# A two-layer graph kernel on one core: VectorE reads TensorE's results at later places in its order

## The chip, the core and the metric

The kernel runs on one core of a Trainium2 chip. A core has five engines that work beside each other: TensorE (PE in the profile; PEld is its weight load), VectorE (DVE), ScalarE (ACT), GpSimd (POOL) and SyncE (SP, which issues DMAs). Each engine runs its own instructions in order and waits, at an instruction, for semaphores of the others. The metric is the device time of one execution in microseconds. Three timed runs of the kernel before gave 2594.83 us as median (2593.11 to 2597.05).

## What is computed

The reference takes 3125 nodes with 256 features, 103125 edges sorted by destination (with self loops), and two layers. Cut to its end:

```python
xn = _layernorm(x, axis=-1)
x = x + _L0_gnn_ref(xn, src, dst, ...) + _L0_mix_ref(xn[None], ...)[0]
x = x + _L0_ffn_ref(_layernorm(x, axis=-1)[None], ...)[0]
xn = _layernorm(x, axis=-1)
x = x + _L1_gnn_ref(xn, src, dst, edge_type_8, ...) + _L1_mix_ref(xn[None], ...)[0]
x = x + _L1_ffn_ref(_layernorm(x, axis=-1)[None], ...)[0]
return x
```

- `_L0_gnn_ref` takes, for each node, the maximum over its incoming edges of a linear map of the source row. `_L0_mix_ref` is a linear attention: `q` and `k` have their mean over the features taken off, are squared and normalised; `kv` is a sum over all nodes. `_L0_ffn_ref` routes all tokens to the same two of eight experts (one decision from the mean of all rows), with a layer norm behind.
- `_L1_gnn_ref` sums, for each node, rows of the table "node x relation" over its edges. `_L1_mix_ref` is another linear attention. `_L1_ffn_ref` is a mixture of eight experts in which every token takes two; the kernel computes all eight and weighs each with a share that is zero for six of them.

## The kernel before

**Tiles and passes.** The nodes are sorted by their number of edges and cut into 25 tiles of 128. For tile `t`, `STEPS[t]` gathers fetch one source row for each of its 128 nodes; there are 814 gathers in a pass. `edge_pass` (L1241 and on) is run twice. Pass 1 (layer 0, maximum) gathers from `btab`, pass 2 (layer 1, sum) from `htab_f`. Ahead of pass 1 lies a stage that sorts and builds tables; between the passes lies the table stage (`Four`), which ends layer 0 and writes `htab_f`.

**What a pass does.** POOL issues the gathers (L179) in chunks of up to four into tiles `gt` from a pool of 6 (pass 1) or 5 (pass 2) buffers. VectorE folds a chunk (L1264) and adds it to the tile's accumulator (L1269; L1267 for a tile's first chunk). This frees the buffer for POOL.

**The order of everything else.** A queue `bg` holds jobs with a cost each. After each chunk the pass gives itself credit, a rate times the number of gathers, and takes jobs off `bg` while there is credit. The rate is the cost in `bg` by the gathers left in the group of tiles, held between the two values of `pace`. The order of VectorE's and POOL's instructions is exactly that of the program (`manual_schedule`); TensorE's and ScalarE's are placed by the scheduler, so a job's matmuls can begin before VectorE gets to the job's own instructions. But where a VectorE instruction needs a product, everything behind it on VectorE waits too, the folding of gathers among it.

**The jobs of pass 1.** First the mixing: `nodes_in` normalises five tiles, `mix_tile` is a generator with four stages (products; means and squares; sums over nodes; scaling and transposes), of which `mix_step(i)` runs one stage of each of four tiles, `i-3` to `i`. At the end of each group of tiles (`GROUPS`, mostly three tiles) `after0` appends that group's `Fin0` jobs (end of the first sublayer: `products`, `sums`, `norms`). From group 3 (`SURE`) on, when the two experts have been guessed from the nodes seen so far (`guess`), it also appends `hidden` (first expert matmuls and gelus), `outputs_a` (second matmuls, into one PSUM bank `py` for a tile) and `outputs_b`. The last lets ScalarE copy the first expert's half out of `py` (L1452), and VectorE add the second's to the token row and take it off the copy (L1453, L1454). `settle` later finds the true weights.

**The jobs of pass 2.** First attention: `att_k`, `att_softmax`, 25 times `att_ctx`, then `att_end`, in which VectorE reads the sum `pctx` (L1981). Then for each group of tiles a `Group`: ten small jobs (sums, norms, routing), ten jobs `step(i)` for the eight experts, and an end. `step(i)` runs `hidden(i)` (matmuls L2120, gelus L2124, and L2126, which spreads the row of shares of expert `i` over the partitions in PSUM, `wb`), `share(i-1)` (VectorE multiplies the gelus by `wb`, L2134) and `outputs(i-2)` (L2149). A group's last three steps and its end are dealt out between the first small jobs of the next group (`late`).

Of the kernel before, what the change touches and what calls it, by code (L numbers as in the profile page):

```python
# [11 lines left out]
F32 = mybir.dt.float32  # L12
# [44 lines left out]
SEEN = GROUPS[SURE][-1]  # L57

# [18 lines left out]
def gps_kernel(ctx: ExitStack, tc: tile.TileContext, a, out):  # L77
# [1155 lines left out]
    def fast():  # L1233
# [168 lines left out]
        hTs, pys = {}, {}  # L1402
# [41 lines left out]

        def outputs_b(ts):


            for t in ts:
                py = pys.pop(t)
                y = py.rearrange("p (i c n) -> p i c n", i=2, c=2)  # L1450
                d = xT[:, :, t * P : (t + 1) * P]
                S.copy(d, y[:, 0, :, :])  # L1452
                V.tensor_tensor(xt_tok[:, t, :], xt_tok[:, t, :], py[:, D:], op=ALU.add)  # L1453
                V.tensor_tensor(d, d, y[:, 1, :, :], op=ALU.subtract)  # L1454
# [12 lines left out]
        with ExitStack() as l0x:  # L1467
# [48 lines left out]
            w_qkv = mat_load("w_qkv", a["m0_qkv"], m0w, 3 * D)  # L1516
            b_qkv = row_load("b_qkv", a["m0_bqkv"], 3 * D, m0w)
# [5 lines left out]
            def nodes_in(g):  # L1523

                ask(5 * g + 5)
                yield
                mv = small.tile([P, 5, 2], F32, name="mv5")
                rs = small.tile([P, 5], F32, name="rs5")
                fetch(5 * g + 5)
                for j in range(5):  # L1530
                    stats(x[:, 5 * g + j, :], mv[:, j, :])
                V.tensor_scalar(rs, mv[:, :, 1], EPS, None, op0=ALU.add)
                S.activation(rs, rs, AF.Sqrt)
                yield
                V.reciprocal(rs, rs)
                for j in range(5):
                    xn = work.tile([P, D], F32, name="xn")
                    normalize(xn, x[:, 5 * g + j, :], mv[:, j, :], rs[:, j : j + 1])
                    to_xT(5 * g + j, xn)
# [5 lines left out]
            def mix_tile(t):  # L1545
# [7 lines left out]
                tok_mm(pvv[:, :D], w_qkv[:, :, 512:], t, stop=False)  # L1553
                PE.matmul(pvv[:, :D], ones_row, b_qkv[:, 512:], start=False, stop=True)
                yield
                nm = small.tile([P, 2], F32, name="nm")
                V.reduce_sum(nm, pq.rearrange("p (h d) -> p h d", h=2), axis=AX.X)
                V.tensor_scalar(nm, nm, -1.0 / D, None, op0=ALU.mult)
                ss = small.tile([P, 2], F32, name="ss")
                q2 = m0.tile([P, D], F32, name="q2", bufs=3)  # L1560
                k2 = m0.tile([P, D], F32, name="k2", bufs=3)
                S.activation(q2, pq[:, :D], AF.Square, bias=nm[:, 0:1], accum_out=ss[:, 0:1])
                S.activation(k2, pq[:, D:], AF.Square, bias=nm[:, 1:2], accum_out=ss[:, 1:2])
                vs = m0.tile([P, D], F32, name="vs", bufs=3)
                S.copy(vs, pvv[:, :D])
# [129 lines left out]
            nodes = [staged(nodes_in(g), (1.0, 4.0, 6.0)) for g in range(5)]  # L1695
# [3 lines left out]
            def mix_step(i):  # L1699
                for back in (3, 2, 1, 0):  # L1700
                    if 0 <= i - back < NT:
                        next(mixing[i - back], None)

            for i in range(NT + 3):
                bg.append((7.0 if i < NT else 3.0, lambda i=i: mix_step(i)))
                if i % 5 < 3 and i // 5 + 1 < 5:
                    bg.append(nodes[i // 5 + 1][i % 5])
            bg.extend(staged(mix_end(), (2.0, 3.0, 1.0)))

            def after0(g, tiles, accs):  # L1710
# [5 lines left out]
                if g == SURE:  # L1716
                    bg.extend(staged(guess(), (2.0, 1.0, 1.0, 1.0, 1.0, 1.0)))
                    for r in range(NX):
                        bg.extend(staged(relation(r), (1.5, 1.5)))
                for ts in GROUPS[: g + 1] if g == SURE else [tiles] if g > SURE else []:  # L1720
                    bg.append((5.0 * len(ts), lambda ts=ts: hidden(ts)))
                    bg.append((4.0 * len(ts), lambda ts=ts: outputs_a(ts)))
                    bg.append((1.0 * len(ts), lambda ts=ts: outputs_b(ts)))
# [4 lines left out]
            fin = []  # L1728
# [8 lines left out]
            with tc.manual_schedule(engines={mybir.EngineType.DVE, mybir.EngineType.Pool}):  # L1737
                edge_pass(
                    gp, btab[:], idx1, ALU.max, bg, after0, GROUPS, 4, (1.3, 1.3), None,
                    lambda t: accp.tile([P, D], F32, name="acc"), ahead,  # L1740
                )
                while bg:
                    bg.popleft()[1]()
# [3 lines left out]
            with tc.manual_schedule(engines={ET.DVE, ET.Pool, ET.PE, ET.Activation}):  # L1747
# [10 lines left out]
                outputs_a(ts)  # L1758

        again = nc.values_load(missed[0:1, 0:1])  # L1760
        with tc.If(again > 0):
# [8 lines left out]
            for ts in GROUPS:  # L1770
# [10 lines left out]
                outputs_a(ts)  # L1781
                if ts != GROUPS[-1]:
                    outputs_b(ts)
# [114 lines left out]
        with ExitStack() as l1x:  # L1898
# [101 lines left out]
            class Group:  # L2000
# [113 lines left out]
                def hidden(self, e):  # L2114
                    n, at0 = self.n, self.at0
                    hT = self.hT[e] = f1.tile([P, FC, 4 * P], F32, name="hT1")
                    for f in range(FC):
# [6 lines left out]
                        S.activation(hT[:, f, :n], ph[:, :n], AF.Gelu, bias=b1[:, e, f : f + 1])  # L2124
                    wb = self.wb[e] = ps_tr.tile([P, 512], F32, name="pt")
# [54 lines left out]
                def step(self, i):  # L2180

                    if i < NX:
                        self.hidden(i)
                    if 1 <= i <= NX:
                        self.share(i - 1)
# [39 lines left out]
            for t in range(NT):  # L2225
                bg.append((1.7, lambda t=t: att_ctx(t)))
                if t % 5 == 0:
                    bg.append((0.0, lambda e=t // 5: load_expert(e, wp)))
            bg.append((6.0, att_end))
# [120 lines left out]
```

## Time and profile before

| | us |
|---|---|
| timed median of 3 | 2594.83 |
| the profiled execution's own time | 3147.58 |
| its span | 3145.9 |
| first and last gather of pass 1 | 128.5, 1463.4 |
| first and last gather of pass 2 | 1716.6, 3056.2 |
| POOL busy, VectorE busy, TensorE busy | 1767.0, 1272.5, 1950.3 |

The profiled execution took 553 us more than the timed ones, so lengths read from it are its own and are not those of a timed run. In the lines of the profile a group of instructions is named by line, engine, operation and tiles; "[32.04 <-DVE acc L1269]" means that the engine was idle for 32.04 us ahead of the instruction, and that VectorE's result of line 1269 came last. "issue" is idle time in which nothing was waited for that the profile shows, and "remote" is a releaser that it can't name. The granted clock of TensorE averages 0.764 of full speed.

### The profile page before, as it was taken

What the parts mean: (1) busy time and instruction counts of PE and PEld (TensorE: products, weight loads), DVE (VectorE), ACT (ScalarE), POOL (GpSimd) and SP (SyncE); (2) the same over time, 40 slices, a digit from 0 to 9 for tenths busy, and PEclk for the clock granted to TensorE, in tenths of its full rate; (3) what the DMA queues carried; (4) which work ended last, traced back from release to release, by engine and by line L of the source; (5) the groups of instructions that cost most, each with busy time, mean ns of one, the idle gap of its engine ahead of it and who ended that gap; (6) DMA issues with size and microseconds to landing.
All of it is one profiled execution on the core that took longest, in us unless ns stands there. A gap on an engine that the chain in (4) does not pass through costs nothing.

```text
span 3145.9 us, 20994 instructions
## 1 busy us (share of the span) xinstructions
PE 1950.3 (62%) x6146; PEld 1123.0 (36%) x6146; DVE 1272.5 (40%) x3135; ACT 543.2 (17%) x1272; POOL 1767.0 (56%) x1850
## 2 busy tenths in 40 slices
PE   2446577205553515256897155587887788787888
PEld 1323243103332303134343144232333344554667
DVE  5635445336224232224552233443534254343442
ACT  2213220001110101012121131111212021221233
POOL 4365656675656474742344737675556655565650
PEclk8668777557766757577898567688988889888979
DMA  5332323233222232321478533232222222232220
GB/s 162 103 93 81 94 74 107 88 103 100 87 80 84 61 102 62 103 62 35 186 300 308 157 95 93 88 98 84 77 76 87 87 82 84 78 90 81 81 73 15
DMA packets 129367, 314.68 MB, mean 100 GB/s; under 512 B 39520, under 2 KB 64166, under 8 KB 122836
## 3 DMA queue, kind: packets, MB, share of 16 engines
q0 software_dynamic: 86784, 252.60, 26.8%
q1 hardware_dynamic: 36526, 56.36, 5.1%
q10 hardware_dynamic: 5926, 4.21, 0.5%
q8 instruction: 53, 0.87, 0.1%
q14 instruction: 78, 0.64, 0.1%
HBM read 246.35 MB, written 66.69 MB: 100 GB/s over the span
## 4 chain that ended last, share of the span: by engine, by line
PE 26%; issue 9%; another core or an unknown queue 6%; DVE 5%; DMA 3%; POOL 3%; ACT 2%; ACTq 0%; POOLq 0%; DVEq 0%
PE mm L2120 9%; PE py L2149 8%; PE mm L174 4%; POOL gt L179 2%; DMA htab_f<-hs,id_i 2%; PE pt L2126 2%; DVE gt L1264 1%; PE mm L2089 1%; DVE bnst L148 1%; PE mm L2014 1%; ACT L2124 0%; ACT hT L2124 0%; DVE acc L1269 0%; PE pt L2082 0%
## 5 line engine op out<-in xcount | busy, mean ns | idle before, releaser
L179 POOL DMA_INDIRECT gt<-htab_f,idx2g x814 | 797.5, 980 | 527.4 <-DVE acc L1269 269.7
L179 POOL DMA_INDIRECT gt<-btab,idx x814 | 799.9, 983 | 510.6 <-issue 224.7
L1264 DVE TENSOR_TENSOR gt<-gt 128x256 f32<-128x256 f32 (+1 forms) x831 | 444.4, 535 | 334.6 <-DMA gt<-btab,idx 149.8
L2120 PE MATMUL mm<-xT,w 128*128 128x256 f32 (+4 forms) x1408 | 403.6, 437 | 87.9 <-issue 63.4
L2149 PE MATMUL py<-hT,w 128*128 128x256 f32 (+4 forms) x1408 | 407.4, 439 | 78.2 <-issue 77.1
L2120 PEld LDWEIGHTS mm<-xT,w 128*128 128x128 f32 x1408 | 253.4, 208 | 233.4 <-issue 155.1
L2149 PEld LDWEIGHTS py<-hT,w 128*128 128x128 f32 x1408 | 250.5, 205 | 228.1 <-issue 187.6
L2134 DVE TENSOR_TENSOR hT<-hT,pt 128x1024 f32<-128x1024 f32 (+4 forms) x88 | 117.5, 1336 | 422.8 <-ACT hT L2124 241.1
L2124 ACT ACTIVATE hT<-mm,b 128x256 f32<-128x256 f32 (+4 forms) x352 | 167.9, 496 | 677.6 <-PE mm L2120 234.6
L1411 PE MATMUL mm<-xT,w 128*128 128x384 f32 (+2 forms) x320 | 125.1, 556 | 155.9 <-issue 110.3
L174 PE MATMUL mm<-w_rel,xT 128*128 128x512 f32 x400 | 183.6, 618 | 5.1 <-ACT xT L169 3.3
L1269 DVE TENSOR_TENSOR acc<-acc,gt 128x256 f32<-128x256 f32 x403 | 172.2, 427 | 35.0 <-DVE gt L1264 13.2
L174 PE MATMUL pt<-w_own,xT 128*128 128x256 f32 x100 | 44.4, 580 | 207.5 <-issue 113.8
L1411 PEld LDWEIGHTS mm<-xT,w 128*128 128x128 f32 x320 | 72.0, 251 | 208.9 <-issue 139.5
L1453 DVE TENSOR_TENSOR xt<-xt,mm 128x256 f32<-128x256 f32 x25 | 10.5, 420 | 308.1 <-ACT xT L1452 302.3
L1440 PE MATMUL mm<-w,hT 128*128 128x256 f32 x400 | 105.4, 413 | 29.1 <-issue 27.3
L174 PE MATMUL mm<-w_qkv,xT 128*128 128x512 f32 (+1 forms) x200 | 96.0, 596 | 41.7 <-issue 41.5
L174 PEld LDWEIGHTS mm<-w_rel,xT 128*128 128x128 f32 x400 | 77.9, 198 | 103.0 <-issue 87.1
L174 PEld LDWEIGHTS pt<-w_own,xT 128*128 128x128 f32 x100 | 25.6, 285 | 222.8 <-issue 121.1
L1440 PEld LDWEIGHTS mm<-w,hT 128*128 128x128 f32 x400 | 79.2, 204 | 66.9 <-issue 53.9
L1674 PE MATMUL pmean<-ones,xt 128*128 128x1 f32 (+1 forms) x100 | 23.5, 339 | 115.9 <-DVE xt L157 70.1
L226 POOL DMA_INDIRECT htab_f<-hs,id_i x25 | 25.1, 1003 | 97.6 <-DMA htab_f<-hs,id_i 34.6
(391 smaller groups left out, 2181.9 us busy)
## 6 DMA issues: line engine op xcount, KB each, us to landing
here<-hs SPq DMA_DIRECT2D x25, 1024.0 KB
gt<-btab,idx POOLq DMA_INDIRECT x814
gt<-htab_f,idx2g POOLq DMA_INDIRECT x814
w<-in_f_W_dram SPq DMA_DIRECT2D x20, 512.0 KB
ntab<-x SPq DMA_DIRECT2D x5, 640.0 KB
btab<-bs SPq DMA_DIRECT2D x5, 640.0 KB
otab<-xn SPq DMA_DIRECT2D x25, 128.0 KB
acc<-otab SPq DMA_DIRECT2D x25, 128.0 KB
```

The costliest lines, as they stand in the source:

```text
L148: V.bn_stats(out=st, in_=src)
L174: PE.matmul(ps, lhs[:, c, t * P : (t + 1) * P], w[:, c, :], start=start and c == 0, stop=stop and c == 1)
L179: G.indirect_dma_start(out=dst, out_offset=None, in_=table, in_offset=bass.IndirectOffsetOnAxis(ap=idx, axis=0))
L1264: V.tensor_tensor(gt[:, :h, :], gt[:, :h, :], gt[:, m - h : m, :], op=op)
L1269: V.tensor_tensor(acc, own(t) if i == 0 else acc, gt[:, 0, :], op=op)
L1411: PE.matmul(ph[:, :n], w1[:, i, c, f * P : (f + 1) * P], xT[:, c, at0 : at0 + n], start=(c == 0), stop=(c == 1),)
L1440: PE.matmul(py[:, i * D : (i + 1) * D], hTs[i][:, f, j * P : (j + 1) * P], w2[:, i, f, :], start=False, stop=(f == FC - 1), skip_group_che ...
L2120: PE.matmul(ph[:, :n], w1s[e][:, c, f * P : (f + 1) * P], xT[:, c, at0 : at0 + n], start=(c == 0), stop=(c == 1),)
L2124: S.activation(hT[:, f, :n], ph[:, :n], AF.Gelu, bias=b1[:, e, f : f + 1])
L2126: PE.matmul(wb[:, :n], ident[:NX, e : e + 1].to_broadcast([NX, P]), self.wT[:, :n], start=True, stop=True)
L2134: V.tensor_tensor(hT[:, :, :n], hT[:, :, :n], wb[:, None, :n].to_broadcast([P, FC, n]), op=ALU.mult)
L2149: PE.matmul(self.py[c][:, :n], w2s[e][:, f, c * P : (c + 1) * P], hT[:, f, :n], start=False, stop=(e == NX - 1 and f == FC - 1),)
```

## The change

Five things are edited.

1. `outputs_b` is split. A new `outputs_out` lets ScalarE copy both halves of `py` out of PSUM, the second into an SBUF tile `y1` (six buffers, and one of its own for tile 0). `outputs_b` then only has the two VectorE instructions, which read `y1`. In `bg` it is put off: a list `waiting` holds it, and it is queued behind the next group's `hidden`.
2. `mix_tile` has three stages instead of four, run two steps apart (`i-4`, `i-2`, `i`). The means of `q` and `k` come out of the products: `w_qkv` and `b_qkv` get two more columns, the negative means of their own columns, so VectorE's reduction L1557 and scale L1558 go. The squares move into the first stage. `nodes_in` hands out its five normalisations one by one.
3. The costs of `guess` are raised, and the pace of pass 1 goes from (1.3, 1.3) to (0.9, 1.3).
4. In `Group`, the row of shares is spread by a job of its own, `weigh`, one step later, and `share` runs one step later too, ahead of `hidden`.
5. In pass 2 an empty job of cost 20 stands ahead of `att_end`.

The diff, cut to its core:

```diff
+SECONDS = 6
...
+        def outputs_out(ts):
             for t in ts:
                 py = pys.pop(t)
-                y = py.rearrange("p (i c n) -> p i c n", i=2, c=2)
+                if t == 0:
+                    y1 = seconds[t] = seconds[t] if t in seconds else f0h.tile([P, D], F32, name="y1_0", bufs=1)
+                else:
+                    y1 = seconds[t] = f0h.tile([P, D], F32, name="y1", bufs=SECONDS)
+                S.copy(xT[:, :, t * P : (t + 1) * P], py[:, :D].rearrange("p (c n) -> p c n", c=2))
+                S.copy(y1, py[:, D:])
+
+        def outputs_b(ts):
+            for t in ts:
+                y1 = seconds.pop(t)
                 d = xT[:, :, t * P : (t + 1) * P]
-                S.copy(d, y[:, 0, :, :])
-                V.tensor_tensor(xt_tok[:, t, :], xt_tok[:, t, :], py[:, D:], op=ALU.add)
-                V.tensor_tensor(d, d, y[:, 1, :, :], op=ALU.subtract)
+                V.tensor_tensor(xt_tok[:, t, :], xt_tok[:, t, :], y1, op=ALU.add)
+                V.tensor_tensor(d, d, y1.rearrange("p (c n) -> p c n", c=2), op=ALU.subtract)
...
+            w_qkv = m0w.tile([P, 2, 3 * D + 2], F32, name="w_qkv")
...
+            for m in range(2):
+                at = slice(3 * D + m, 3 * D + m + 1)
+                V.reduce_sum(w_qkv[:, :, at], w_qkv[:, :, m * D : (m + 1) * D], axis=AX.X)
+                V.tensor_scalar(w_qkv[:, :, at], w_qkv[:, :, at], -1.0 / D, None, op0=ALU.mult)
+                V.reduce_sum(b_qkv[:, at], b_qkv[:, m * D : (m + 1) * D], axis=AX.X)
+                V.tensor_scalar(b_qkv[:, at], b_qkv[:, at], -1.0 / D, None, op0=ALU.mult)
...
                 for j in range(5):
+                    if j:
+                        yield
                     xn = work.tile([P, D], F32, name="xn")
...
-                tok_mm(pvv[:, :D], w_qkv[:, :, 512:], t, stop=False)
-                PE.matmul(pvv[:, :D], ones_row, b_qkv[:, 512:], start=False, stop=True)
-                yield
-                nm = small.tile([P, 2], F32, name="nm")
-                V.reduce_sum(nm, pq.rearrange("p (h d) -> p h d", h=2), axis=AX.X)
-                V.tensor_scalar(nm, nm, -1.0 / D, None, op0=ALU.mult)
+                tok_mm(pvv[:, : D + 2], w_qkv[:, :, 512:], t, stop=False)
+                PE.matmul(pvv[:, : D + 2], ones_row, b_qkv[:, 512:], start=False, stop=True)
...
-                S.activation(q2, pq[:, :D], AF.Square, bias=nm[:, 0:1], accum_out=ss[:, 0:1])
-                S.activation(k2, pq[:, D:], AF.Square, bias=nm[:, 1:2], accum_out=ss[:, 1:2])
-                vs = m0.tile([P, D], F32, name="vs", bufs=3)
-                S.copy(vs, pvv[:, :D])
+                S.copy(vs, pvv[:, : D + 2])
+                S.activation(q2, pq[:, :D], AF.Square, bias=vs[:, D : D + 1], accum_out=ss[:, 0:1])
+                S.activation(k2, pq[:, D:], AF.Square, bias=vs[:, D + 1 :], accum_out=ss[:, 1:2])
                 yield
...
-            nodes = [staged(nodes_in(g), (1.0, 4.0, 6.0)) for g in range(5)]
+            nodes = [staged(nodes_in(g), (1.0, 4.0) + 5 * (1.2,)) for g in range(5)]
...
-                for back in (3, 2, 1, 0):
+                for back in (4, 2, 0):
...
-            for i in range(NT + 3):
+            for i in range(NT + 4):
                 bg.append((7.0 if i < NT else 3.0, lambda i=i: mix_step(i)))
-                if i % 5 < 3 and i // 5 + 1 < 5:
-                    bg.append(nodes[i // 5 + 1][i % 5])
+                if i // 5 + 1 < 5:
+                    a0, a1 = ((0, 1), (1, 2), (2, 3), (3, 5), (5, 7))[i % 5]
+                    bg.extend(nodes[i // 5 + 1][a0:a1])
...
-                    bg.extend(staged(guess(), (2.0, 1.0, 1.0, 1.0, 1.0, 1.0)))
+                    bg.extend(staged(guess(), (4.0, 3.0, 3.0, 2.0, 2.0, 2.0)))
...
                     bg.append((5.0 * len(ts), lambda ts=ts: hidden(ts)))
-                    bg.append((4.0 * len(ts), lambda ts=ts: outputs_a(ts)))
-                    bg.append((1.0 * len(ts), lambda ts=ts: outputs_b(ts)))
+                    if waiting:
+                        bg.append(waiting.pop())
+                    bg.append((4.0 * len(ts), lambda ts=ts: (outputs_a(ts), outputs_out(ts))))
+                    waiting.append((1.0 * len(ts), lambda ts=ts: outputs_b(ts)))
+                if g == len(GROUPS) - 2:
+                    bg.append((4.0, lambda: None))
+                    bg.append(waiting.pop())
...
-                    gp, btab[:], idx1, ALU.max, bg, after0, GROUPS, 4, (1.3, 1.3), None,
+                    gp, btab[:], idx1, ALU.max, bg, after0, GROUPS, 4, (0.9, 1.3), None,
...
+                def weigh(self, e):
+                    n = self.n
                     wb = self.wb[e] = ps_tr.tile([P, 512], F32, name="pt")
...
+                    if 2 <= i <= NX + 1:
+                        self.share(i - 2)
                     if i < NX:
                         self.hidden(i)
                     if 1 <= i <= NX:
-                        self.share(i - 1)
+                        self.weigh(i - 1)
                     if i >= 2:
                         self.outputs(i - 2)
...
+            bg.append((20.0, lambda: None))
             bg.append((6.0, att_end))
```

## The prediction

> **What bounds the kernel now.** I read the page first (busy shares and the costliest groups), then the waits of the whole run, then the timeline around the longest stalls.
>
> ```profile
> PE 1950.3 (62%) x6146; PEld 1123.0 (36%) x6146; DVE 1272.5 (40%) x3135; ACT 543.2 (17%) x1272; POOL 1767.0 (56%) x1850
> ...
> L179 POOL DMA_INDIRECT gt<-htab_f,idx2g x814 | 797.5, 980 | 527.4 <-DVE acc L1269 269.7
> L179 POOL DMA_INDIRECT gt<-btab,idx x814 | 799.9, 983 | 510.6 <-issue 224.7
> ```
>
> No engine is full. The reader is to see that POOL's two lots of 814 gathers have idle time before them nearly as long as themselves.
>
> ```profile
> POOL gt L179 <- DVE acc L1269: 483.9, 74, 36.1
> ...
> DVE xt L1453 <- ACT xT L1452: 302.3, 19, 41.9
> ...
> DVE hT L2134 <- ACT hT L2124: 241.1, 18, 33.4
> ...
> DVE hT L2134 <- PE pt L2126: 97.1, 38, 16.8
> ...
> DVE cx L1981 <- PE pctx L1977: 51.1, 1, 51.1
> ```
>
> The columns are total, times, longest. POOL waits for gather buffers, which VectorE frees at L1269; VectorE, in order, stands at a result of TensorE (outputs_b L1453, share L2134, att_end L1981). One such place, from the timeline:
>
> ```profile
> 1053.42 0.95 POOL L179 DMA_INDIRECT gt<-btab,idx  x1 [0.30 <-issue]
> 1054.68 0.95 POOL L179 DMA_INDIRECT gt<-btab,idx  x1 [0.30 <-issue]
> ...
> 1075.94 0.42 DVE L1453 TENSOR_TENSOR xt<-xt,mm 128x256 f32<-128x256 f32 x1 [41.35 <-ACT xT L1452]
> ...
> 1087.67 1.15 POOL L179 DMA_INDIRECT gt<-btab,idx  x1 [32.04 <-DVE acc L1269]
> ```
>
> An undisturbed gather takes 0.95 us and comes every 1.25 us (0.30 of "issue"); VectorE stands 41.35 us, POOL then 32.04.
>
> **The budget.** Pass 1's gathers start from 128.5 to 1463.4 us: 836 intervals (814 gathers, 23 table rows, less one) at 1.25 us are 1045 of 1335, so 290 us of stall. Pass 2 starts from 1716.6 to 3056.2: 829 intervals (813, 2 own rows, 14 output scatters) at 1.25 are 1036 of 1340, so 303. Together 593. Without any stall the profiled execution would span 3145.9 - 593 = 2553 us, with the 1.7 us that lie around the span 2555. But the timed median is 2594.8, against 3147.6 for the profiled execution. If gathers come every 1.25 us there too, only 40 us of stall are left in the timed runs; if they come every 0.95, 1665 x 0.30 = 500 more. This is the largest unknown here. A second view speaks for a small budget:
>
> ```profile
> 2293.23 1.01 PE L2149 MATMUL py<-hT,w 128*128 128x512 f32 x1 [1.79 <-issue]
> ...
> 2296.03 1.01 PE L2149 MATMUL py<-hT,w 128*128 128x512 f32 x1 [1.79 <-issue]
> ...
> 2303.77 2.42 ACT L2124 ACTIVATE hT<-mm,b 128x512 f32<-128x512 f32 x4 [38.96 <-remote]
> 2306.23 2.29 DVE L2134 TENSOR_TENSOR hT<-hT,pt 128x2048 f32<-128x2048 f32 x1 [33.37 <-ACT hT L2124]
> ```
>
> TensorE does 16 such matmuls in 7.1 us elsewhere; here they come 2.8 us apart with nothing waited for, while POOL issues, and run on as soon as POOL stops. Such crawls stand behind many of the long VectorE waits. If they belong to the recording, they are absent in a timed run; the trace can't say. I take a real budget of 150 us: 40; some 60 because the stages outside the passes (469 us) hold the same kind of gap (23.8 us before L168 at 166 us, 17.7 before L1954 at 1717) and should be shorter too; and 50 for a gather that is 0.03 us quicker.
>
> **What the Trainium skill says.** "Perfetto Trace Analysis", Summary: the profiler window per engine type: a TensorE record ends at an estimate. The trace agrees: matmuls of L1411 recorded from 1034.6 reach ACT only at 1050.3. "TensorE: Matmul & The Clock Gate", Part 1: an idle array falls to half clock and is released by activity. Here the granted clock is 0.50 from 600 to 700 us, where TensorE idles, and 1.00 from 1076 to 1086, so TensorE's work costs up to double where it is thin. "Perfetto Trace Analysis", Optimizing Scalar/DVE Operations, gives VectorE more access time on PSUM than on SBUF (about 125 against 60 ns). Here L1453 from PSUM takes 420 ns and L1269 from SBUF 427, so reading y1 from SBUF saves nothing. Same page, Matmuls: evacuation of one PSUM bank should overlap the next group's matmuls; freeing py with two ACT copies helps that way, though no wait of before names it alone.
>
> **Part by part, in the profiled execution's time.**
>
> Outputs a group later. ACT gains 50 copies of 256 columns at 372 ns (row of L1452): 18.6 us over pass 1, where ACT is at most a tenth busy from 560 us on (42.5 of 470 us from 1000 to 1470); the cover is that idle time. The adds move: counted in VectorE's order in both builds, those of tiles 10 to 12 stand after gather chunk 173 of 428 instead of 148, some 25 chunks x 5 us later; in the burst after guess 4 to 13 chunks later. TensorE needed at most 42 us. So L1453's waits go, and with them POOL's stalls behind them: 11.95 + 6.25 + 25.48 + 32.04 + 31.29 + 31.58 + 18.73 + 5.19 = 162 us. Next is POOL's own cadence. Bounds: 100 (TensorE's crawl returns at Fin0's sums) to 162; I take 162, as the sums come a group of 93 gathers after.
>
> Mixing. VectorE loses 25 reductions (681 ns) and 25 scales (197 ns): 22 us, on an engine that is under half busy there, so hidden; it gains eight small set-up operations, under 3 us, which wait for w_qkv beside weights that land at 137 us. TensorE's V product gains 2 columns on 256: nothing. The first VectorE touch of a tile moves from one mix step after its products to two, the last from three to four, and nodes_in's five tiles are dealt out one by one (waits for L168: 34.8 us). POOL's stalls from 128 to 505 us sum to 64. Half stays, since the same in-order chain remains: 32 saved, bounds 0 to 64.
>
> Guess and pacing. Dearer steps spread the routing chain over more chunks: half of the 15.6 us before 736.6, so 8. The pace from 0.9 instead of 1.3 moves jobs later within a group; each group still empties, so 0, between -10 and +10 for a colder clock.
>
> att_end 20 units later, six chunks (226 to 232): the wait of 51.1 us and POOL's 36.1 behind it go. The first group's routing moves with it by 30 us and has caught up by the second (chunk 263 in both).
>
> Shares two steps. This is the doubtful part. share(e) now stands where share(e+1) stood. But its row of weights comes from weigh(e), which TensorE now does after hidden(e+1). So at the same place VectorE needs the same matmuls done as before; only ACT's last gelu (0.69 us and its hand-over, 1.7 in all) is spared. In return TensorE's outputs(e) waits for a share one step nearer: it may run ahead of VectorE by one step, not two. At a group's end share(6), behind gelus(2,4), gates outputs(6), which was free before: four adds (1.6 us) and the share (2.3), less the weigh product (1.1), about 3 us of TensorE. Over ten such ends 30 us at most; half of them where TensorE is the limit, less some gelus saved: I charge 8, bounds -30 (gain) to +40.
>
> POOL's and SP's instructions keep their order, so no queue is passed. The sum: 162 + 32 + 8 + 36 = 238 of 593 us of stall, 40%. As the profiled stall is larger than the timed one, I carry the share over, not the microseconds: 0.40 x 150 = 60, less 8 for the shares, which is not scaled: 52. 2594.8 - 52 is 2543 us.
>
> **The rivals.**
> B, the stalls are real: gathers come faster unprofiled, say every 1.10 us; the budget is 40 + 0.15 x 1665 = 290, of which 40% is 116: 2479 us (2380 to 2510). For it: the crawls begin and end with POOL's gathers, which a timed run has as well. Against: VectorE's small operations follow each other within 0.05 us under the same recording, so the 0.30 is POOL's own.
> C, no change: VectorE's waits without crawls fit into the 20 to 24 gathers of buffer (25 to 30 us), POOL never starves but where TensorE is full (7 to 9 tenths from 2050 on), which the change leaves: 2593 us.
> D, slower: TensorE is the limit in pass 2 and outputs wait for shares. 4 us lost at each of ten group ends, plus a quarter-step (4 us) in ten places where TensorE can't run ahead: 80 in the worst case, about 40 with half, against some 15 gained in pass 1: 2620 us. It decides from the point where a group loses more than a tenth of pass 1's gain (3 us). For it: PE hidden and outputs lead the chain (9% and 8%). Against: pass 2 keeps 303 us in which POOL waits, not TensorE.
> That the edit fails to move VectorE's work is ruled out by the order.
>
> **Numbers.** Forecast A, 2543 (2510 to 2588): 0.45. B 0.21, C 0.14, D 0.20. This kernel's measurement can tell about 0.2% (5 us). Faster is A and B, 0.66; within, C, 0.14; slower, D, 0.20. The range 2450 to 2615 leaves out a third of B and half of D.
>
> **What would show it.** In the changed profile L1453's successor waits under 30 us in all, not 302; POOL's stalls of 25 to 32 us between 950 and 1440 are gone; att_end's wait is under 10; share waits stay above 200 us with the releaser now PE's weigh product, and TensorE's outputs wait for VectorE. I am wrong if the share waits vanish, if the timed gain passes 85 us (stalls are real), or if TensorE's idle time in pass 2 grows by more than pass 1 gains.

## The result, and the profile after

| | us |
|---|---|
| before, median of 20 runs beside the change | 2591.47 (2585.28 to 2597.05) |
| after, median of 20 runs | 2597.1 (2588.69 to 2599.5) |
| ratio, 95% interval | 1.0017 (1.0009 to 1.0025) |
| after, the profiled execution's span | 2595.8 |

The changed kernel is 0.17% slower, about 4.4 us (the medians lie 5.6 us apart). The interval leaves out 1, so this is a small loss, but by the bound of 0.2% that the prediction set it is no change. The forecast was 2543. Runs of these kernels fell at two levels of time, where the kernel before takes 2595 or 3155 us; only runs of one level are compared, and unless the text says otherwise it is the first.

This time the profiled execution takes as long as the timed ones. First the page of after: busy time by engine, then the two groups of gathers with their idle time before and what ended it.

```profile
PE 1802.9 (69%) x6146; PEld 1077.6 (42%) x6146; DVE 1258.8 (48%) x3093; ACT 551.3 (21%) x1297; POOL 1765.7 (68%) x1850
...
L181 POOL DMA_INDIRECT gt<-htab_f,idx2g x814 | 799.1, 982 | 270.0 <-issue 219.3
L181 POOL DMA_INDIRECT gt<-btab,idx x814 | 796.5, 978 | 249.8 <-issue 222.1
```

The idle time before the gathers has halved against the first profile of before (527.4 and 510.6), and almost all that is left are the 0.30 us between two gathers, which the profile mostly calls "issue" and which are part of the cadence. The view of waits for the same run (total, times, longest):

```profile
DVE hT L2164 <- PE pt L2156: 163.0, 50, 9.9
...
PE py L2179 <- DVE hT L2164: 43.7, 13, 18.9
...
PE mm L2009 <- DVE cx L2007: 27.6, 1, 27.6
POOL gt L181 <- DVE acc L1271: 26.0, 30, 12.0
```

POOL now waits 26.0 us for gather buffers, not 483.9. VectorE does not wait at all at the successor of L1453, nor at att_end; in att_end it is TensorE that waits for VectorE. Read against the first profile of before, 458 us of stall are gone, and yet the timed kernel is no faster. So the first thing to ask is whether that profile shows what the timed runs did.

### The profile page after: what moved, and what is told of

Read it like the earlier page. It is cut to its first block, busy times and chain, and to the rows that moved or that the text cites. A ratio compares the mean times of both kernels' runs of the same rounds, so it can differ in the third digit from the quotient of the medians.

```text
span 2595.8 us, 20939 instructions
## 1 busy us (share of the span) xinstructions
PE 1802.9 (69%) x6146; PEld 1077.6 (42%) x6146; DVE 1258.8 (48%) x3093; ACT 551.3 (21%) x1297; POOL 1765.7 (68%) x1850
## 4 chain that ended last, share of the span: by engine, by line
PE 25%; POOL 9%; issue 8%; DVE 5%; DMA 4%; ACT 1%; POOLq 0%; DVEq 0%; ACTq 0%
POOL gt L181 9%; PE py L2179 8%; PE mm L2146 8%; PE mm L176 6%; DMA gt<-htab_f,idx2g 2%; DVE gt L1266 1%; DMA htab_f<-hs,id_i 1%; PE pt L2156 1%; PE mm L2115 1%; PE mm L2040 1%; DVE bnst L150 1%; DVE acc L1271 0%; DMA out_dram<-x,id_i 0%; DVE hT L2164 0%; ACT L2150 0%
## 5 line engine op out<-in xcount | busy, mean ns | idle before, releaser
L2179 PE MATMUL py<-hT,w 128*128 128x256 f32 (+4 forms) x1408 | 383.0, 429 | 43.7 <-DVE hT L2164 43.7
L2146 PE MATMUL mm<-xT,w 128*128 128x256 f32 (+4 forms) x1408 | 373.6, 417 | 12.6 <-DVE x L2046 10.2
L2179 PEld LDWEIGHTS py<-hT,w 128*128 128x128 f32 x1408 | 245.0, 201 | 176.7 <-issue 82.1
L2146 PEld LDWEIGHTS mm<-xT,w 128*128 128x128 f32 x1408 | 240.6, 197 | 137.7 <-issue 87.0
L176 PE MATMUL pt<-w_own,xT 128*128 128x256 f32 x100 | 39.0, 523 | 260.2 <-DVE acc L1675 260.2
L2164 DVE TENSOR_TENSOR hT<-hT,pt 128x1024 f32<-128x1024 f32 (+4 forms) x88 | 117.4, 1334 | 163.0 <-PE pt L2156 163.0
L1413 PE MATMUL mm<-xT,w 128*128 128x384 f32 (+2 forms) x320 | 95.3, 464 | 16.5 <-DMA w<-in_f_W_dram 16.5
L1442 PE MATMUL mm<-w,hT 128*128 128x256 f32 x400 | 93.0, 386 | 0.8 <-ACT hT L1434 0.8
L176 PE MATMUL mm<-w_qkv,xT 128*128 128x512 f32 (+1 forms) x200 | 85.9, 552 | 0.5 <-ACT xT L171 0.5
L1413 PEld LDWEIGHTS mm<-xT,w 128*128 128x128 f32 x320 | 64.0, 222 | 47.2 <-DMA w<-in_f_W_dram 15.3
```

The source lines that it names most:

```text
L176: PE.matmul(ps, lhs[:, c, t * P : (t + 1) * P], w[:, c, :], start=start and c == 0, stop=stop and c == 1)
L1413: PE.matmul(ph[:, :n], w1[:, i, c, f * P : (f + 1) * P], xT[:, c, at0 : at0 + n], start=(c == 0), stop=(c == 1),)
L1442: PE.matmul(py[:, i * D : (i + 1) * D], hTs[i][:, f, j * P : (j + 1) * P], w2[:, i, f, :], start=False, stop=(f == FC - 1), skip_group_che ...
L2146: PE.matmul(ph[:, :n], w1s[e][:, c, f * P : (f + 1) * P], xT[:, c, at0 : at0 + n], start=(c == 0), stop=(c == 1),)
L2164: V.tensor_tensor(hT[:, :, :n], hT[:, :, :n], wb[:, None, :n].to_broadcast([P, FC, n]), op=ALU.mult)
L2179: PE.matmul(self.py[c][:, :n], w2s[e][:, f, c * P : (c + 1) * P], hT[:, f, :n], start=False, stop=(e == NX - 1 and f == FC - 1),)
```

## Experiments

### The kernel before, profiled again

No edit.

> The kernel before, unchanged, for a second profile of it. Theory 1 (the long waits of the first profile belong to that one execution): the span is 2585 to 2600 us like the timed runs, gathers come every 1.25 us, POOL's stalls over both passes are under 80 us in all (593 in the first profile) and VectorE waits under 60 us at L1453 (302 there). Theory 2 (the waits are there in the timed runs too, and the change trades those of pass 1 for new ones in pass 2): pass 1 is longer than the changed kernel's 1072 us by 20 us or more, pass 2 is shorter than its 1083 by as much.

Measured: 2594.7 us, ratio 1.0005 (0.9992 to 1.0018), span 2599.5. Its view of waits, the lines that answer to the ones above:

```profile
DVE hT L2134 <- PE pt L2126: 153.2, 50, 9.9
...
PE py L2149 <- DVE hT L2134: 58.0, 2, 45.7
...
POOL gt L179 <- DVE acc L1269: 24.4, 34, 11.1
...
DVE xt L1453 <- ACT xT L1452: 11.7, 3, 6.8
...
PE mm L1983 <- DVE cx L1981: 11.1, 1, 11.1
```

The kernel before has no such stalls either: 24.4 us at the gather buffers, 11.7 where the first profile had 302.3, none at L1981. Its gathers start from 109.8 to 1184.8 us and from 1437.7 to 2517.1, so the passes take 1075.0 and 1079.4 us. With 836 and 828 intervals at 1.25 us (1045 and 1035) this leaves 30 and 44 us. After has 27 and 48 (1071.9 and 1082.6 us). The sum is 74 before and 75 after.

Most of that is not waiting. The 1.25 us are made from a median gather of 0.95 us; the mean gather takes 0.98, and over 1628 gathers the difference is 53 us in both kernels. Counted one by one, POOL waits for VectorE in pass 1 never longer than the 0.30 us that lie between any two gathers, in both kernels. In pass 2 the kernel before has two such waits, 14.7 us together:

```profile
1866.79 1.16 POOL L179 DMA_INDIRECT gt<-htab_f,idx2g  x1 [3.61 <-DVE acc L1269]
...
1980.24 1.15 POOL L179 DMA_INDIRECT gt<-htab_f,idx2g  x1 [11.09 <-DVE acc L1269]
```

After has them too, a little longer:

```profile
1865.44 1.15 POOL L181 DMA_INDIRECT gt<-htab_f,idx2g  x1 [5.33 <-DVE acc L1271]
...
1979.34 1.15 POOL L181 DMA_INDIRECT gt<-htab_f,idx2g  x1 [12.05 <-DVE acc L1271]
```

In pass 1, where the larger part of the change lies, it finds nothing to remove, and in pass 2 it removes nothing. The timeline of after at 1000 us shows both engines at work:

```profile
1000.74 0.94 POOL L181 DMA_INDIRECT gt<-btab,idx  x1 [0.30 <-issue]
1001.98 0.94 POOL L181 DMA_INDIRECT gt<-btab,idx  x1 [0.30 <-issue]
1003.23 0.94 POOL L181 DMA_INDIRECT gt<-btab,idx  x1 [0.30 <-issue]
1004.16 1.15 DVE L1266 TENSOR_TENSOR gt<-gt 128x512 f32<-128x512 f32 x2 [4.09 <-DMA gt<-btab,idx]
```

POOL keeps its 1.25 us; VectorE is the one that waits, for the gathers.

### One part at a time

Outputs alone on the kernel before (`outputs_out` split off, `outputs_b` put off through `waiting`); the shares alone on it; and the change without its shares. The order of a step in the kernel before with the shares alone, as a diff:

```diff
+                    if 2 <= i <= NX + 1:
+                        self.share(i - 2)
                     if i < NX:
                         self.hidden(i)
                     if 1 <= i <= NX:
-                        self.share(i - 1)
+                        self.weigh(i - 1)
                     if i >= 2:
                         self.outputs(i - 2)
```

> The kernel before with the second expert's outputs a group later and nothing else of the change. Theory 1: within 2 us of before, ratio 0.9993 to 1.0007, as POOL never starved there. Theory 2: pass 1 gains 20 us or more, about 2570 us, ratio 0.992.

> The kernel before with the shares two steps later and nothing else of the change. Theory 1 with the shares as the cost: 2594 to 2598 us, ratio 1.001 to 1.0025. Theory 2: 2610 us or more, as pass 2 loses what pass 1 gains. If shares are free: 2591, ratio within 0.0005 of 1.

> The changed kernel with share and the spreading of its weights back at their old steps (share(i-1) behind hidden(i)). Theory 1, with the shares as the cost: the changed kernel's 0.17% go, 2590 to 2593 us, ratio to before 0.999 to 1.0005. Theory 2: pass 2 gives back 20 us or more, about 2570 us, ratio 0.992. If the loss comes from elsewhere (pace, the later att_end, pass 1): it stays near 2597, ratio 1.0015 to 1.002.

| kernel | ratio to before | 95% interval |
|---|---|---|
| before, outputs later | 1.0012 | 1.0000 to 1.0024 |
| before, shares later | 1.0021 | 1.0012 to 1.0031 |
| after, shares at their old steps | 1.0001 | 0.9988 to 1.0015 |

The shares alone cost as much as the whole change, and without them the change costs nothing that can be measured. Outputs alone, at 1.0012, lie above the 0.9993 to 1.0007 that were expected, but their interval reaches from nothing to a loss of 0.24%: whether they cost anything stays open. Mixing, guess with pace, and att_end were not run alone.

### Where in pass 2 the shares cost it

The new order once in all groups but the last three, once (with `< 3`) in the last three only, which are those of tiles 2, 1 and 0. Against the kernel before with the shares alone:

```diff
+                    late = self.tiles[0] >= 3
-                    if 2 <= i <= NX + 1:
+                    if late and 2 <= i <= NX + 1:
                         self.share(i - 2)
                     if i < NX:
                         self.hidden(i)
+                        if not late:
+                            self.weigh(i)
                     if 1 <= i <= NX:
-                        self.weigh(i - 1)
+                        if late:
+                            self.weigh(i - 1)
+                        else:
+                            self.share(i - 1)
```

> The kernel before, with weigh and share two steps behind hidden in all groups of pass 2 but the last three (those of tiles 0, 1 and 2 keep the old order). With the new order in all groups the ratio was 1.0021. Theory E: the loss arises early, where TensorE waits for a share (in the trace of all groups at the new order, some 8 us between 1700 and 2100 us), and it can't be caught up, because TensorE is 92 to 100% busy from 1700 us to the end: ratio 1.0015 to 1.0025. Theory T: the loss arises in the tail, where the last groups run one after the other with no gathers left: ratio 1.000, within 0.0008.

> The kernel before, with weigh and share two steps behind hidden in the last three groups of pass 2 only (tiles 0, 1 and 2). Theory E (the loss arises in the early groups): ratio 1.000, within 0.0008. Theory T (the loss arises in the tail, one step of share and one wait for it per group): ratio 1.0015 to 1.0025. If each is half right, both runs give about 1.001.

Measured 1.0027 (1.0017 to 1.0037) and 1.0003 (0.9988 to 1.0018). The loss is in the first eight of the eleven groups, not in the last three. The busy time of POOL by stretches (start and end, length, busy with count, then clock and DMA) of the kernel before:

```profile
1800.00:1900.00 100.00, 73.53 (x77) 0.89 0.36 104
1900.00:2000.00 100.00, 68.19 (x70) 0.97 0.34 95
sum 200.00, POOL 141.73; mean POOL 70.86
```

and of the one with the new order in the first eight groups:

```profile
1800.00:1900.00 100.00, 71.21 (x73) 0.89 0.35 100
1900.00:2000.00 100.00, 68.00 (x69) 0.96 0.34 95
sum 200.00, POOL 139.21; mean POOL 69.61
```

A stretch of 100 us without a stall holds 76.2 us of POOL. This is the one place of pass 2 where POOL waits for VectorE for longer than a moment (the two waits shown above), and there VectorE stands at TensorE's products: in the kernel before 35.8 us at the sums L2019 and 46.6 at the shares between 1800 and 2000 us, the longest of them, 15.9, just ahead of POOL's 11.1. The new order takes 2.5 us of POOL's work from it. At 0.95 us of work in 1.25 this is 3.3 us of time, about half of this run's loss. These are single profiles, but they agree: with the new order the sum is 140.8 (shares alone), 140.0 and 138.7 (after, twice), with the old one 141.6 (after, shares at their old steps), 141.8 (only the last three groups changed) and 141.7 (outputs alone). POOL's waits for VectorE in pass 2 of more than 0.5 us say the same: 14.7 to 15.0 us in the four profiles with the old order in these groups, 16.3 to 19.2 in the four with the new one. That is 1 to 5 us of a loss of 4 to 7; the profiles don't show where the rest lies.

TensorE waits for shares more as well. In the kernel before these were two waits at the start of pass 2 (58.0 us, above); with the shares alone there are 16:

```profile
PE py L2153 <- DVE hT L2138: 82.4, 16, 41.9
```

In after with its shares at their old steps there is none, in after 43.7 us in 13. Most of the new ones are 1 to 3 us long.

### Half the gather buffers

```diff
-tc.tile_pool(name="gp0", bufs=6)
+tc.tile_pool(name="gp0", bufs=3)
...
-tc.tile_pool(name="gp1", bufs=5)
+tc.tile_pool(name="gp1", bufs=3)
```

> The kernel before with 3 gather buffers in each pass instead of 6 and 5, that is 10 to 12 gathers or some 14 us of work ahead of VectorE instead of 20 to 24 gathers or 25 to 30 us. Theory 1 (the buffers hide VectorE's waits for TensorE, which are below 20 us each): with 3 of them some waits show, POOL stalls more often, 2620 to 2680 us, ratio 1.01 to 1.033. Rival (the waits are too short to matter at any depth that still lets POOL run ahead): ratio below 1.003.

> The changed kernel with 3 gather buffers in each pass instead of 6 and 5. Theory 1 (the change takes VectorE's waits away, and the full buffers had hidden them): slower than with full buffers, but 5 to 30 us faster than the kernel before with 3 buffers. Rival (what shows with few buffers is VectorE's own work in long jobs, which the change doesn't shorten): as slow as the kernel before with 3 buffers, within 5 us. If 3 buffers are enough, both stay within 0.3% of 2594 us and the pair tells nothing.

Measured 2620.4 us, 1.0096 (1.0066 to 1.0126), for before, and 2625.3, 1.0114 (1.0088 to 1.0140), for after. The first expectation holds, the second fails, and the rival to it (within 5 us) holds: the change does not help when buffers are few. The gathers of the kernel before with 3 buffers (count, shortest/median/longest in ns, first and last start) say why:

```profile
L179 POOL DMA_INDIRECT gt<-btab,idx x814: 940/946/1442, 109.5 to 1182.2; - x163
L179 POOL DMA_INDIRECT gt<-htab_f,idx2g x814: 940/946/1466, 1433.7 to 2541.6; - x163
```

Pass 1 takes 1072.7 us with 3 buffers and 1075.0 with 6: in the pass in which the outputs and the mixing lie, even half the buffers hide all that VectorE waits for. The whole loss is in pass 2 (1107.9 for 1079.4), where POOL's longer waits for VectorE are 47.3 us instead of 14.7; in pass 1 they are 2.3. That VectorE's own work in long jobs is what shows there was not tested.

### Is it POOL? Fewer gathers

```diff
+FEWER = 4
-                left = sum(STEPS[t] for t in tiles)
+                left = sum(STEPS[t] - FEWER for t in tiles)
...
-                    for i, (k0, k1) in enumerate(chunks(STEPS[t], most)):
+                    for i, (k0, k1) in enumerate(chunks(STEPS[t] - FEWER, most)):
```

> The kernel before with the last four gathers of every tile left out in both passes (100 of 814 a pass), so four of each node's edges are not counted. Theory 1 (POOL's gather cadence of 1.25 us bounds both passes): 200 x 1.25 = 250 us less, 2345 us, ratio 0.904. Rival (TensorE, 92 to 100% busy from 1700 us on, bounds pass 2): pass 1 loses 125 us, pass 2 with its tail 0 to 30, so 2440 to 2470 us, ratio 0.940 to 0.952.

> The changed kernel with the same four gathers of every tile left out in both passes. Theory 1: as the kernel before with fewer gathers, within 8 us, since VectorE's waits still fit into the gather buffers. Rival (once POOL has less to do, the waits that the change takes away would show): 10 to 40 us faster than the kernel before with fewer gathers. If TensorE then bounds pass 2, the later shares cost more than 5 us, and it is slower than the kernel before with fewer gathers by 5 to 15 us.

> The kernel before with the last four gathers of every tile left out in both passes, once more, for a place where the kernel before takes 2595 us. Theory 1 (POOL's cadence of 1.25 us bounds both passes): 2345 us, ratio 0.904. Rival (TensorE bounds pass 2 from 1700 us on): 2440 to 2470 us, ratio 0.940 to 0.952. Where the kernel before takes 3155 us: 0.924 again, since 200 gathers at 1.25 us are 250 us, of which 236 were measured.

The first pair was a surprise of another kind. The unchanged kernel, run beside it, took 3155.04 us there, not 2595, and the profile of the kernel before with fewer gathers has all the stalls of the first profile (464.5 us at the gather buffers, 302.4 at the line that was L1453). So that profile was no accident of recording: there are times or places at which this kernel takes 3155 us, timed as well as profiled, and all timed runs that were made together fell at one level. The pair gave 2919.4 us, 0.9242 (0.9196 to 0.9288), for before and 2910.6, 0.9216 (0.9157 to 0.9275), for after, too close to tell them apart.

The repeat fell at 2595 us: 2401.7 us, ratio 0.9256 (0.9234 to 0.9279), 195 us less for 200 gathers. Between the 250 of theory 1 and the 125 to 155 of the rival. Its gathers:

```profile
L181 POOL DMA_INDIRECT gt<-btab,idx x714: 942/949/1432, 108.2 to 1056.4; - x179
L181 POOL DMA_INDIRECT gt<-htab_f,idx2g x714: 942/949/1427, 1302.7 to 2294.0; - x179
```

Pass 1 takes 948.2 us, 127 less: 100 gathers at 1.27, which is the mean gather of 0.98 us and the 0.30. There POOL alone is the bound. Pass 2 takes 991.3, 88 less, and its tail 103.6 for 82.4 us: 67 of 125 are left. There TensorE is close behind POOL: VectorE stands 226.4 us at the row of shares (153.2 in the kernel before) and 100.1 at the sums (65.4), and POOL waits some 60 us for VectorE (14.7). So both theories are half right, each in one pass. (The "92 to 100% busy" is too high at the low end: TensorE's share is 82 to 100% in the stretches of 100 us from 1700 to 2500.) The changed kernel with fewer gathers was run only where the kernel before takes 3155 us; whether it would gain at 2595 us once POOL has less to do stays open.

### The change at the other level

> The changed kernel as it is, beside the kernel before on the same chip. The two runs with fewer gathers fell where the kernel before takes 3155 us, as in its first profile, with the same crawls of TensorE; all other runs fell where it takes 2595 us. Theory 1: at 2595 us the ratio is 1.001 to 1.003, as measured. At 3155 us VectorE's waits are longer than the gather buffers, so the change has something to remove: if the forecast's working holds there, 238 of 593 us of stall go, ratio 0.92 to 0.94. Rival (the next use of the same late TensorE products, the sums of Fin0, takes the waits over): ratio 0.99 to 1.00, as the pair with fewer gathers hints (2919 against 2911 us).

> The changed kernel as it is, once more. Where the kernel before takes 2595 us: ratio 1.001 to 1.003. Where it takes 3155 us: 0.92 to 0.94 if the working of the forecast holds there; 0.99 to 1.00 if the sums of Fin0 and the gelus take over the waits that the change removes.

The first fell at 2595: 1.0020 (1.0009 to 1.0031), as before. The second fell beside a kernel before of 3159.77 us: 3096.25 us (four runs, 3075 to 3124), ratio 0.9825 (0.9777 to 0.9874), a gain of about 55 us (40 to 70; the medians lie 63 apart) and neither the 0.92 to 0.94 of the working nor the 0.99 to 1.00 of the rival. Its gathers take 1283.5 us in pass 1 (1334.9 in the first profile of before) and 1318.8 in pass 2 (1339.6). The view of waits:

```profile
POOL gt L181 <- DVE acc L1271: 410.7, 69, 28.6
...
PE mm L1442 <- issue: 157.9, 59, 9.8
DVE acc L1675 <- PE pt L176: 156.8, 5, 45.8
...
DVE xt L1464 <- ACT y L1456: 43.1, 3, 20.5
...
DVE acc L1675 <- PE mm L1671: 38.5, 1, 38.5
...
DVE cx L2007 <- PE pctx L2003: 36.4, 1, 36.4
```

The 302.3 us at L1453 have become 43.1 at its successor L1464. But TensorE, which was late with the expert matmuls, is late with the next products in its order as well: VectorE now stands at the sums of Fin0, L1675, for 156.8 + 38.5 us and up to 45.8 at a time (213.8 in all; 23.1 at the same line, L1657, in the first profile of before). What makes TensorE late has not gone: its idle time with no visible cause adds up to 612 us in the first profile of before and to 632 here. It has moved, from the first expert matmuls (110.3 us there, 31.6 here) to the second (27.3 there, 157.9 here). POOL's stall falls by 73 us (483.9 to 410.7), not by 162; the two profiled executions lie 72 us apart.

Two more profiles of changed kernels at this level, of the next section, agree on L1464 (44.7 and 47.5 us). They don't on att_end: with the empty job it waits 36.4, 50.3 and 51.0 us, without it 51.1, 50.6, 35.1 and 35.0. The six chunks have no effect that can be seen.

### The order within a step, and the pace of pass 2

These five fell at the 3155 level, though the first three were meant for the other.

```diff
-                    if 2 <= i <= NX + 1:
-                        self.share(i - 2)
                     if i < NX:
                         self.hidden(i)
                     if 1 <= i <= NX:
                         self.weigh(i - 1)
+                        self.share(i - 1)
```

(b_share_after is the kernel before with this order, a_share_after the changed kernel with it; a_share_back_again is the changed kernel with weigh and share both at their old steps.) For the pace, in the call of `edge_pass` for pass 2:

```diff
-GROUPS1, 4, (0.9, 1.3), lambda t: inits[t],
+GROUPS1, 4, (0.9, 1.7), lambda t: inits[t],
```

> The kernel before, with weigh one step later (as in the change) but share(i-1) still in step i, right behind weigh(i-1). If the loss of the new order is that TensorE's outputs wait for a share that now stands one step nearer to them, this run has no loss: ratio 1.000, within 0.001. If it is the row of shares that comes later, and VectorE stands at the share for it, the loss stays: 1.0015 to 1.003.

> The kernel before with the upper pace of pass 2 raised from 1.3 to 1.7, so that attention and the first group's jobs are taken off the queue sooner. Theory E (TensorE's late start in pass 2 stalls VectorE and POOL by some 15 us from 1800 to 2000 us): 3 to 12 us gained, ratio 0.995 to 0.999. Rival (the stall is set by when TensorE gets through the first groups, whatever the queue does, or jobs that bunch up stall POOL elsewhere): 1.000 to 1.004.

> The same with the upper pace at 2.5. Theory E: as with 1.7 or a little more, 0.993 to 0.999. Rival: slower than with 1.7, since VectorE takes more jobs between two chunks and meets TensorE's results before they are there: 1.002 to 1.01.

> The changed kernel with share(i-1) put back into step i, right behind weigh(i-1); the row of shares stays one step later. Where the kernel before takes 2595 us: ratio 1.000, within 0.001, if the loss came from shares a step nearer to the outputs; 1.0015 to 1.003 if it came from the later row. Where it takes 3155 us: if the 0.7% that this order alone gained adds to what the rest of the change gains, 0.970 to 0.980; if not, as the changed kernel, 0.980 to 0.985.

> The changed kernel with weigh and share at their old steps. Where the kernel before takes 2595 us: ratio 1.000, as measured before. Where it takes 3155 us: 0.980 to 0.985 if outputs, mixing and att_end bring the whole of the gain of 63 us there; 0.985 to 0.992 if the later shares bring a third to a half of it.

| kernel, beside before at 3158 to 3160 us | median us | ratio | 95% interval |
|---|---|---|---|
| before, weigh later, share behind it | 3138.89 | 0.9933 | 0.9908 to 0.9958 |
| before, pace 1.7 | 3162.89 | 1.0007 | 0.9987 to 1.0027 |
| before, pace 2.5 | 3163.40 | 1.0013 | 0.9988 to 1.0038 |
| after (from above) | 3096.25 | 0.9825 | 0.9777 to 0.9874 |
| after, share behind weigh | 3090.24 | 0.9794 | 0.9754 to 0.9833 |
| after, shares at old steps | 3114.01 | 0.9856 | 0.9804 to 0.9909 |

At this level outputs, mixing, pacing and att_end together bring some 45 of the 55 us (0.9856), and the shares perhaps the rest, though the intervals overlap. The later row of weights helps here even alone (0.9933). "After, share behind weigh" is the fastest in the table but can't be told from after, and it was not run at 2595 us. The pace of pass 2 makes no difference that these runs can tell (0.4%). Whether the faster pace or the order within the step would win back the 4 to 5 us at the 2595 level wasn't measured: no run of them fell there.

## Why the prediction was wrong

**The step that failed is the size of the budget**: "I take a real budget of 150 us: 40; some 60 because the stages outside the passes [...] hold the same kind of gap [...] and 50 for a gather that is 0.03 us quicker." At the 2595 level POOL waits 14.7 us for VectorE, all of it in pass 2. None of the three parts is there as a stall that the change could take away:

- The gather is no quicker: 0.949 us in the median and 0.30 of issue at both levels, and in the mean 0.98 at both.
- The stages outside the passes, 471 us in the first profile, are 445 in before_again (109.8 + 252.9 + 82.4), so they give 26 us and not 60. The two gaps that were named stay: the longest before L168 is 21.6 us for 23.8, before L1954 17.7 for 17.7.
- The 40 are no stall: they come from a cadence that counts the median gather, and the mean one uses them up (53 us over both passes).

**The step behind it failed too**: "I carry the share over, not the microseconds: 0.40 x 150 = 60." A share of stall can only be carried over if the same waits make up the small stall and the large one. They don't. At 2595 us the waits which the change addresses are gone or hold nobody up: 11.7 us at L1453 with no POOL wait behind them, none at att_end; and the 153.2 at the row of shares have become 163.0. The removable share was none, and the 60 us were 0. This was rival C in its own words ("VectorE's waits without crawls fit into the 20 to 24 gathers of buffer"), with a chance of 0.14, and the working had held the evidence for it: it noted that the profiled execution took 553 us longer than the timed ones, and that at an unchanged cadence 40 us were left. It then raised the 40 to 150 on two guesses. The crawls do not belong to the recording, a question that it left open: timed runs at 3155 us are as slow as that profile. But the change was timed at the other level.

**Smaller slips in the sums.** Pass 2 has 828 intervals and not 829 (13 output scatters lie between the first gather and the last). The stages outside the passes are 471 us, not 469. ScalarE gains 25 copies, not 50 (1272 instructions before, 1297 after). The idle time before the gathers is about two thirds of their own length (527.4 of 797.5 us), not nearly as long. None of these moves the forecast by more than a few us.

**Shares: sign right, size near.** Charged 8 us with bounds of -30 and +40; measured +5.4 alone (0.21% of 2595), and it decides the sign of the whole. The mechanism is in part as the prediction had it. It named outputs that wait for a share one step nearer, about 3 us at the ends of groups, "half of them where TensorE is the limit". The runs put the loss into the first eight groups of pass 2 and not into the last three, and with the shares alone TensorE waits 24.4 us more for shares (82.4 for 58.0), some of it at ends of groups: 2.18 us before the last two outputs at 1827 us and again at 1974. But waits of 0.8 to 3.2 us lie inside the first groups as well, and that these waits of TensorE make up the loss isn't shown. Which part of the order costs it, the later row or the later share, stays open too. Rival D had the right sign at a fifth of its 25 us.

**Outputs.** "L1453's waits go, and with them POOL's stalls behind them", 162 us in the profiled execution's time, with 100 as lower bound for a crawl that "returns at Fin0's sums". At the 3155 level, the only one with these waits, they went from 302.3 to 43.1 us, and at Fin0's sums the waiting rose from 23.1 to 213.8 us. All of pass 1, with the mixing's 32 and the guess's 8, gained 51 us, not 202. The mechanism of the lower bound was the one that came, and still its number was too high.

**Mixing, guess, pace.** Not measured alone. At 2595 us they make, together with outputs and att_end, nothing that can be told (after with its shares put back: 1.0001, 0.9988 to 1.0015). VectorE's busy time fell by the 22 us that were said (1281.1 to 1258.8), and they were hidden, as said.

**att_end.** "The wait of 51.1 us and POOL's 36.1 behind it go." At 2595 us there was no such wait; at 3155 us it was 36.4 to 51.0 us with the change and 35.0 to 51.1 without.

**The marks named beforehand.** L1453's successor under 30 us: yes, none at all, but before had 11.7. POOL's stalls of 25 to 32 us gone: yes, but before had none over 11.1. att_end under 10: yes, but before had none. Share waits above 200 us with the weigh product as releaser: only 163.0; the releaser is right, but in before_again it was the same, with 153.2. TensorE's outputs wait for VectorE: yes, 43.7 us. Three of five came true without any effect of the change, since the comparison was with a profile of another level.

## What to carry to other kernels

Compare the span of the profile with the timed median before reading anything else; where they differ by a fifth, the waits of the profile aren't those of the timed runs, and no share of them may be carried over. What stays the same in both (here the cadence of one engine) gives the budget: count its intervals, take them off the length of the stage, and believe the small remainder. Count them at the mean length of an instruction, not the median: here 0.03 us a gather made 53 us of "stall" that nobody waited for. And list the waits of the bounding engine one by one; two of them, 14.7 us, were all that VectorE cost it. And where an engine waits for another that is late as a whole, moving one wait back uncovers the next one: of some 260 us of waits taken away at one line, 73 us of stall went and about 55 us of time.

## What the runs showed of the hardware

The same kernel takes 2595 us at some times and 3155 at others, and timed runs made together were always at one level. The number of the chip does not decide it: chip 12 gave 2596 us for the kernel before at one time and 3158 at a later one.

POOL's gathers don't differ between the levels (0.949 us in the median, 0.30 between). Nor does the stage between the passes: 253.2 us in the first profile of before, 252.9 in before_again, at a granted clock of 0.89 and 0.90. The two passes take 260 us longer each. There TensorE differs: its idle time with no visible cause ("issue") is 612 us in the first profile of before and 632 in after at 3096 us, nearly all of it in the passes and none between them, and at the 2595 level there is none at all. The second expert matmuls of layer 0 (busy time and mean ns; idle time before, and what ended it) in after, at 2596 and at 3096 us:

```profile
L1442 PE MATMUL mm<-w,hT 128*128 128x256 f32 x400 | 93.0, 386 | 0.8 <-ACT hT L1434 0.8
```

```profile
L1442 PE MATMUL mm<-w,hT 128*128 128x256 f32 x400 | 141.0, 492 | 176.5 <-issue 157.9 <-ACT hT L1417 18.6
```

What holds TensorE there is not in the traces and stays open. The gaps come in the passes, where POOL gathers; but at the 2595 level the gathers come as densely and there are no gaps, so the gathers alone are not the cause. The mean granted clock of the run differs as well (0.825 in before_again, 0.764 in the first profile), but between the passes it does not, and a clock that is lower where an engine idles more is no proof of a cause. The same change gains 1.75% at one level and loses 0.2% at the other.
